# An image's group norm in one statistics chain, and score maxima taken from the SBUF copy

## The chip, the cores and the metric

The kernel runs on one core of one Trainium2 chip. Its time is the device time of one launch in microseconds; the median of three runs counts. In the text PE is TensorE (matmuls; it loads its weights beside them), DVE is VectorE, ACT is ScalarE, POOL is GpSimd and SP is SyncE, which here only starts transfers. A transfer can also be started from ACT's queue. Each engine works off its own instructions in order and waits on semaphores for the others. SBUF is the working memory of 128 partitions, PSUM holds what matmuls write.

## The reference

Two layers in float32 on an image batch x of 4 x 512 x 32 x 32. The first is a state-space layer; the change does not touch it. The second, cut to what matters (`hw` is 1024):

```python
def _gn(v, G=32, eps=1e-5):                    # group norm: 16 channels x 1024 pixels a group
    g = v.reshape(B_, G, C_ // G, H_, W_)
    m = jnp.mean(g, axis=(2, 3, 4), keepdims=True)
    s = jnp.var(g, axis=(2, 3, 4), keepdims=True)
    return ((g - m) / jnp.sqrt(s + eps)).reshape(v.shape)

def _L1_conv_ref(x, ...):                      # x is already normed by _gn
    x_top    = _conv(x, w_top, b_top, 0)       # 1x1 convolution to 64 channels
    x_center = _conv(x, w_center, b_center, 0) # 1x1 convolution to 64 channels
    x_bottom = _conv(x, w_bottom, b_bottom, 1) # 3x3 convolution, 512 to 512 channels
    ...
    sp_map = jnp.einsum('bnp,bpm->bnm', x_center, x_top)              # 1024 x 1024 scores
    sp_map = jax.nn.softmax(sp_map.reshape(bsz, -1), axis=1)          # one softmax an image
    sp_map = jnp.einsum('bnm,bmc->bnc', sp_map.reshape(...), x_bottom)
    sp_map = sp_map.reshape(bsz, c, h, w)
    return _conv(x + sp_map, w_out, b_out, 1)  # 3x3 convolution, 512 to 512 channels

x = x + _L1_conv_ref(_gn(x), ...)
```

The softmax runs over all scores of an image, so one maximum over 1024 x 1024 values is needed before any of its exponentials.

## The kernel before

The second layer works image by image. `norm` makes the normed image `xg`, `scores` the exponentials `st` of the scores, `conv3` a 3x3 convolution (with weights transformed beforehand, 24 matmul groups named (p, q) for p in 0 to 5 and q in 0 to 3, whose weight tile of 1 MB is loaded for each), `attend` the product of the two, `finish` the sum with the layer's input and the store. The statements are issued by a scheduler that orders each engine's instructions by when their inputs should be there, so that parts that don't depend on each other are interleaved. A pool gives out its tiles by tag in a ring of `bufs` buffers; a new tile waits until the last use of the one it replaces.

The order of an image's stages:

```python
xg = norm(0)
st, rz = scores(0, xg)
for b in range(B):
    xb = conv3(f"b{b}", xg, ub, brow[0])
    after = norm(b + 1) if b + 1 < B else None
    attend(b, xg, st, rz, xb)
    if after is not None:
        st, rz = scores(b + 1, after)
    finish(b, conv3(f"o{b}", xg, uo, brow[1]))
    xg = after
```

The statistics. `chunks` is a list of channel chunks of 128 partitions, `gm_sb` a matrix that averages over the 16 partitions of a group:

```python
def rsqrt(out, var):
    nc.scalar.activation(out, var, AF.Ln, bias=eps)                      # L219
    nc.scalar.activation(out, out, AF.Exp, scale=-0.5)                   # L220

def group_stats(name, chunks, psum, tag):
    n = len(chunks)
    mv = spool.tile([P, n, 2], F32, tag="mv", ...)
    for j, parts in enumerate(chunks):
        bs = spool.tile([P, len(parts), 6], F32, tag="bs", ...)
        for k, part in enumerate(parts):
            nc.vector.bn_stats(bs[:, k, :], part)                        # L229
        nc.vector.bn_aggr(mv[:, j, :], bs)                               # L230
    ...
    pm = psum.tile([P, 512], F32, tag=tag, ...)
    nc.tensor.matmul(pm[:, :n], gm_sb, mv[:, :, 0], start=True, stop=True)   # L235
    nc.vector.tensor_copy(mean, pm[:, :n])                               # L236 gmean
    nc.vector.tensor_sub(dev, mv[:, :, 0], mean)                         # L237 gdev
    nc.vector.tensor_mul(dev, dev, dev)                                  # L238
    nc.vector.tensor_add(dev, dev, mv[:, :, 1])                          # L239
    pv = psum.tile([P, 512], F32, tag=tag, ...)
    nc.tensor.matmul(pv[:, :n], gm_sb, dev, start=True, stop=True)       # L241
    rsqrt(rstd, pv[:, :n])
    return mean, rstd
```

The pools, the norm and the scores of the second layer:

```python
ps = ... tile_pool(name="l1ps", bufs=3, space=PSUM)     # tag "ps": scores, attend, pm, pv, pz
pm = ... tile_pool(name="l1pm", bufs=5, space=PSUM)     # tag "m": the convolutions
xp = ... tile_pool(name="l1x", bufs=2)
fp = ... tile_pool(name="l1f", bufs=3)

def norm(b):
    xg = xp.tile([P, NCC, HH + 2, WW + 2], F32, tag="xg", ...)
    # ... four memsets of the border on POOL ...
    for c in range(NCC):                                                 # NCC = 4
        t = fp.tile([P, L], F32, tag="f4", name=f"x1t_{b}_{c}")          # L = 1024
        for h in range(NH):                                              # NH = 2, T = 512
            nc.scalar.dma_start(                                         # L1046
                t[:, h * T : (h + 1) * T], x1[b][h][c * P : (c + 1) * P, :])
        mean, rstd = group_stats(
            f"l1_{b}_{c}", [[t[:, h * T : (h + 1) * T] for h in range(NH)]], ps, "ps")
        nc.vector.tensor_scalar(                                         # L1052
            xg[:, c, 1 : HH + 1, 1 : WW + 1], ..., mean[:, 0:1], rstd[:, 0:1],
            ALU.subtract, ALU.mult)
    return xg

def scores(b, xg):
    top = fp.tile([PAB, L], F32, tag="f4", ...)
    center = fp.tile([PAB, L], F32, tag="f4", ...)
    # ... 2 x 4 matmuls pt (L1067), copied to center and top by ACT (L1072, L1079) ...
    mx = spool.tile([P, 2 * NMC], F32, tag="mx", ...)                    # NMC = 8
    st = []
    for m in range(NMC):
        t = xp.tile([P, L], F32, tag="st", name=f"st_{b}_{m}", bufs=NMC)
        for h in range(NH):
            pt = ps.tile([P, T], F32, tag="ps", name=f"psc_{b}_{m}_{h}")
            nc.tensor.matmul(pt, top[...], center[...], ...)             # L1088
            nc.scalar.copy(t[:, h * T : (h + 1) * T], pt)                # L1092
            nc.vector.reduce_max(mx[:, 2 * m + h : 2 * m + h + 1], pt, axis=AX.X)   # L1093
        st.append(t)
    nc.vector.reduce_max(mp, mx, axis=AX.X)                              # L1096
    nc.gpsimd.partition_all_reduce(ma, mp, P, bass_isa.ReduceOp.max)     # L1098
    nc.vector.tensor_scalar_mul(ma, ma, -1.0)                            # L1099
    for m in range(NMC):
        nc.scalar.activation(st[m], st[m], AF.Exp, bias=ma,
                             accum_out=rs[:, m : m + 1])                 # L1102
    nc.vector.reduce_sum(rp, rs, axis=AX.X)                              # L1106
    nc.tensor.matmul(pt[:, 0:1], ones, rp, start=True, stop=True)        # L1108 pz
    nc.vector.reciprocal(rz, pt[:, 0:1])                                 # L1110
    return st, rz
```

The convolution, cut to what shares buffers and engines with these:

```python
for pair in PAIRS:                              # (1, 2), (3, 4), (0, 5)
    r = inputs(pair)                            # rr: row transform on POOL, ACT and DVE (L1133 to L1155)
    v = xp.tile([P, NQ, 2, NCC, P], F32, tag="v", name=f"v_{name}_{pair[0]}", bufs=2)
    # ... four DVE tensor_tensor of 128x1024 (L1169 to L1172), one for each q, in the order 2, 1, 0, 3
    for k, p in enumerate(pair):
        for q in (2, 1, 0, 3):
            w = fp.tile([P, NCC, C], F32, tag="u", ..., bufs=3)
            nc.sync.dma_start(w, u[q][p])       # L1178, 1 MB
            m[q] = pm.tile([P, C], F32, tag="m", ...)
            for c in range(NCC):
                nc.tensor.matmul(m[q], v[:, q, k, c, :], w[:, c, :], ...)    # L1182
            # ... for (1, 1) one more with the bias row (L1187) ...
        # ... m[2] is read by ACT (e, L1190), the other three by four DVE instructions (n, L1198)
    # ... POOL adds and subtracts the n of the pair into y (L1202, L1203, L1209, L1210, L1217),
    #     after pair (3, 4) also three DVE instructions (L1218 to L1220)
```

`attend` multiplies `st` with the convolution's y (pat, L1230: 8 groups of 8 matmuls into tag "ps"), and DVE adds each group to `xg` (L1236).

Of the kernel before, what the change touches and what calls it, by code (L numbers as in the profile page):

```python
# [8 lines left out]
F32 = mybir.dt.float32  # L9
AF = mybir.ActivationFunctionType  # L10
ALU = mybir.AluOpType
AX = mybir.AxisListType
# [3 lines left out]
P = 128  # L16
B, C, HH, WW = 4, 512, 32, 32
L = HH * WW
NCC = C // P
# [4 lines left out]
T = 512  # L24
NH = L // T
# [135 lines left out]
def mamba_then_pab_kernel(  # L161
# [25 lines left out]
    nc = tc.nc  # L187
# [3 lines left out]
    spool = ctx.enter_context(tc.tile_pool(name="spool", bufs=2))  # L191
# [20 lines left out]
    x1 = [  # L212
        [dram.tile([C, T], F32, tag=f"x1_{b}_{h}", name=f"x1_{b}_{h}") for h in range(NH)]
        for b in range(B)
# [10 lines that stand above are left out]
        mv = spool.tile([P, n, 2], F32, tag="mv", name=f"mv_{name}")  # L225
        for j, parts in enumerate(chunks):
            bs = spool.tile([P, len(parts), 6], F32, tag="bs", name=f"bs_{name}_{j}")
# [3 lines that stand above are left out]
        mean = spool.tile([P, n], F32, tag="gmean", name=f"gmean_{name}")  # L231
        rstd = spool.tile([P, n], F32, tag="grstd", name=f"grstd_{name}")
        dev = spool.tile([P, n], F32, tag="gdev", name=f"gdev_{name}")
        pm = psum.tile([P, 512], F32, tag=tag, name=f"pm_{name}")
        nc.tensor.matmul(pm[:, :n], gm_sb, mv[:, :, 0], start=True, stop=True)  # L235
        nc.vector.tensor_copy(mean, pm[:, :n])  # L236
        nc.vector.tensor_sub(dev, mv[:, :, 0], mean)  # L237
        nc.vector.tensor_mul(dev, dev, dev)  # L238
        nc.vector.tensor_add(dev, dev, mv[:, :, 1])  # L239
        pv = psum.tile([P, 512], F32, tag=tag, name=f"pv_{name}")  # L240
# [3 lines that stand above are left out]
# [759 lines left out]
    with ExitStack() as l1:  # L1003
        ps = l1.enter_context(tc.tile_pool(name="l1ps", bufs=3, space=PSUM))
# [9 lines left out]
        xp = l1.enter_context(tc.tile_pool(name="l1x", bufs=2))  # L1014
        fp = l1.enter_context(tc.tile_pool(name="l1f", bufs=3))
# [3 lines left out]
        for name, src in (("b", b_bottom), ("o", b_out)):  # L1019
            t = wp.tile([1, C], F32, tag=f"brow_{name}", name=f"brow_{name}")  # L1020
# [12 lines left out]
        NMC = L // P  # L1033
        HR = T // WW

        def norm(b):

            xg = xp.tile([P, NCC, HH + 2, WW + 2], F32, tag="xg", name=f"xg_{b}")
            nc.gpsimd.memset(xg[:, :, 0, :], 0.0)
            nc.gpsimd.memset(xg[:, :, HH + 1, :], 0.0)  # L1040
            nc.gpsimd.memset(xg[:, :, 1 : HH + 1, 0], 0.0)
            nc.gpsimd.memset(xg[:, :, 1 : HH + 1, WW + 1], 0.0)
            for c in range(NCC):
                t = fp.tile([P, L], F32, tag="f4", name=f"x1t_{b}_{c}")
                for h in range(NH):
                    nc.scalar.dma_start(  # L1046
                        t[:, h * T : (h + 1) * T], x1[b][h][c * P : (c + 1) * P, :]
                    )
                mean, rstd = group_stats(
                    f"l1_{b}_{c}", [[t[:, h * T : (h + 1) * T] for h in range(NH)]], ps, "ps"  # L1050
                )
                nc.vector.tensor_scalar(  # L1052
                    xg[:, c, 1 : HH + 1, 1 : WW + 1],
                    t.rearrange("p (h w) -> p h w", w=WW),
                    mean[:, 0:1], rstd[:, 0:1], ALU.subtract, ALU.mult,
                )
            return xg

        def scores(b, xg):


            top = fp.tile([PAB, L], F32, tag="f4", name=f"top_{b}")
            center = fp.tile([PAB, L], F32, tag="f4", name=f"center_{b}")
            for h in range(NH):
                pt = ps.tile([P, T], F32, tag="ps", name=f"pt_{b}_{h}")
                for c in range(NCC):
                    nc.tensor.matmul(  # L1067
                        pt, wt_sb[:, c].rearrange("p j n -> p (j n)"),
                        xg[:, c, 1 + h * HR : 1 + (h + 1) * HR, 1 : WW + 1],
                        start=(c == 0), stop=(c == NCC - 1),  # L1070
                    )
                nc.scalar.activation(  # L1072
                    center[:, h * T : (h + 1) * T], pt[PAB:P], AF.Identity, bias=bt_sb[PAB:P]
                )
                tv = top.rearrange("p (r k i j) -> p r i j k", r=4, k=2, j=TJ)
                pv = pt[0:PAB].rearrange("p (i r j k) -> p r i j k", r=4, j=TJ, k=2)
                hi = slice(h * TI // 2, (h + 1) * TI // 2)
                for r in range(4):
                    nc.scalar.activation(  # L1079
                        tv[:, r, hi], pv[:, r], AF.Identity, bias=bt_sb[0:PAB]  # L1080
                    )
            mx = spool.tile([P, 2 * NMC], F32, tag="mx", name=f"mx_{b}")
            st = []
            for m in range(NMC):
                t = xp.tile([P, L], F32, tag="st", name=f"st_{b}_{m}", bufs=NMC)
                for h in range(NH):
                    pt = ps.tile([P, T], F32, tag="ps", name=f"psc_{b}_{m}_{h}")
                    nc.tensor.matmul(  # L1088
                        pt, top[:, m * P : (m + 1) * P], center[:, h * T : (h + 1) * T],
                        start=True, stop=True,  # L1090
                    )
                    nc.scalar.copy(t[:, h * T : (h + 1) * T], pt)  # L1092
                    nc.vector.reduce_max(mx[:, 2 * m + h : 2 * m + h + 1], pt, axis=AX.X)  # L1093
                st.append(t)
            mp = spool.tile([P, 1], F32, tag="mp", name=f"mp_{b}")
            nc.vector.reduce_max(mp, mx, axis=AX.X)  # L1096
            ma = spool.tile([P, 1], F32, tag="ma", name=f"ma_{b}")
            nc.gpsimd.partition_all_reduce(ma, mp, P, bass_isa.ReduceOp.max)  # L1098
            nc.vector.tensor_scalar_mul(ma, ma, -1.0)  # L1099
            rs = spool.tile([P, NMC], F32, tag="rs", name=f"rs_{b}")  # L1100
            for m in range(NMC):
                nc.scalar.activation(  # L1102
                    st[m], st[m], AF.Exp, bias=ma, accum_out=rs[:, m : m + 1]
                )
            rp = spool.tile([P, 1], F32, tag="rp", name=f"rp_{b}")
            nc.vector.reduce_sum(rp, rs, axis=AX.X)  # L1106
            pt = ps.tile([P, T], F32, tag="ps", name=f"pz_{b}")
            nc.tensor.matmul(pt[:, 0:1], ones, rp, start=True, stop=True)  # L1108
            rz = spool.tile([P, 1], F32, tag="rz", name=f"rz_{b}")
            nc.vector.reciprocal(rz, pt[:, 0:1])  # L1110
            return st, rz
# [129 lines left out]
        def finish(b, y):  # L1241

            dst = out[b].rearrange("(c p) h w -> p c (h w)", p=P)
            for j in range(NCC):
# [19 lines left out]
                nc.scalar.dma_start(dst[:, j, :], o)  # L1264
# [11 lines that stand above are left out]
# [57 lines left out]
```

## Time and profile before

| | |
|---|---|
| median of three runs | 3682.53 us (3678.94 to 3693.1) |
| span of the profiled execution | 3679.3 us |
| first layer | up to about 2450 us |
| second layer | about 1230 us, four images |
| busy over the span: PE, DVE, POOL, ACT | 81%, 67%, 57%, 51% |
| score matmuls psc (L1088), passes x mean | 128 x 0.993 us |
| maxima from PSUM mx (L1093) | 64 x 0.688 us |
| copies st (L1092) | 64 x 0.585 us |
| bn_stats (L229), second layer | 32 x 0.680 us |
| normalisations xg (L1052) | 16 x 0.815 us |
| table loads at L219 and L220, second layer | 15 and 15, mean 1.283 us |

The profile is that of one execution. A group of instructions is named by line, engine, operation and tile, written as out<-in. A float32 matmul stands in it as two passes, so "x768" are 384 matmuls. "Idle before, releaser" says how long an engine stood still ahead of a group, and what ended that. The chain of waits follows the end of the program back from step to step to what released it; it is printed here in order of time. A busy share over the whole span mixes the two layers, so a stage is read from the chain and from the timeline of that stage.

### The profile page before, as it was taken

To read this page: it belongs to the slowest core of one execution; us is meant where nothing else is said; L and a number is where in the kernel's file an instruction comes from. 1 tells how busy PE (TensorE), PEld (TensorE's weight loads), DVE (VectorE), ACT (ScalarE), POOL (GpSimd) and SP (SyncE) were. 2 spreads that over 40 slices of the span, in tenths; PEclk is the share of its full clock that TensorE was granted. 3 is DMA by queue.
4 is the path that set the end of the run, shared out by engine and by line. 5 is a ranking of instruction groups with operands and counts; after the bars stand their busy time and mean duration, and the time that the engine had idled before them with its cause. 6 is when DMAs were issued, how large, how long until landed. Compare 5 with 4: busy or idle time off the path is not lost.

```text
span 3679.3 us, 34763 instructions
## 1 busy us (share of the span) xinstructions
PE 2993.7 (81%) x11208; PEld 1733.5 (47%) x11208; DVE 2465.7 (67%) x2115; ACT 1885.5 (51%) x3567; POOL 2085.2 (57%) x1006
## 2 busy tenths in 40 slices
PE   5878788886688877787887867759889889989988
PEld 3355545554455555445555555523334334434434
DVE  3567878785999987779987788925246435425524
ACT  3487878775768786577775687712130111012000
POOL 6699977685676687666676698912122113113221
PEclk9888898988899888888888988877879979988999
DMA  7588667787667788757777788844418607806817
GB/s 225 171 288 292 231 207 241 242 293 250 231 220 237 246 302 283 244 173 244 255 258 247 276 285 293 302 146 154 149 67 321 228 12 282 316 7 220 331 67 255
DMA packets 378509, 836.38 MB, mean 227 GB/s; under 512 B 33560, under 2 KB 205848, under 8 KB 353496
## 3 DMA queue, kind: packets, MB, share of 16 engines
q1 hardware_dynamic: 367024, 816.50, 64.5%
q10 hardware_dynamic: 11304, 17.67, 1.4%
q8 instruction: 89, 1.46, 0.2%
q14 instruction: 92, 0.75, 0.1%
HBM read 726.57 MB, written 107.48 MB: 227 GB/s over the span
## 4 chain that ended last, share of the span: by engine, by line
PE 46%; DVE 20%; POOL 12%; issue 9%; ACT 7%; DMA 5%; SPq 0%; ACTq 0%; POOLq 0%; DVEq 0%
PE m_o L1182 9%; PE m_b L1182 9%; PE pat L1230 6%; PE y L788 5%; PE po L347 5%; DVE da L768 4%; POOL da L780 3%; PE u L739 3%; PE psc L1088 3%; POOL bbc L754 3%; PE pz L347 3%; DVE bbc L768 2%; PE pxm L347 2%; DVE u L768 2%; ACT sc L725 2%
## 5 line engine op out<-in xcount | busy, mean ns | idle before, releaser
L780 POOL TENSOR_TENSOR da<-da,cbc 128x1024 f32<-128x1024 f32 x256 | 608.5, 2378 | 292.6 <-DVE da L768 244.8
L725 ACT ACTIVATE sc<-dtxt,bt_sb 128x128 f32<-128x128 f32 x2048 | 633.1, 389 | 112.8 <-PE u L739 112.0
L768 DVE TENSOR_TENSOR_SCAN da<-da,u 128x1024 f32<-128x1024 f32 x256 | 582.3, 2275 | 150.4 <-PE u L739 134.6
L754 POOL TENSOR_TENSOR bbc<-dtx,bbc 128x1024 f32<-128x1024 f32 x256 | 607.2, 2382 | 110.2 <-DMA bbc<-bcd 99.9
L739 PE MATMUL u<-ident,sc 128*128 128x128 f32 x2048 | 318.2, 306 | 123.7 <-DVE da L768 72.7
L788 PE MATMUL y<-ident,bbc 128*128 128x128 f32 x2048 | 321.3, 308 | 114.7 <-DVE bbc L775 79.1
L788 PE MATMUL y<-ident,da 128*128 128x128 f32 x2048 | 321.5, 307 | 113.1 <-POOL da L780 109.9
L1182 PE MATMUL m_o<-uw_o,v_o 128*128 128x512 f32 x768 | 354.9, 622 | 23.8 <-DVE v_o L1169 23.2
L788 PEld LDWEIGHTS y<-ident,da 128*128 128x128 f32 x2048 | 270.3, 160 | 198.4 <-POOL da L780 156.2
L780 POOL TENSOR_TENSOR bbc<-bbc,cbc 128x1024 f32<-128x1024 f32 x128 | 306.0, 2391 | 101.2 <-DVE bbc L768 96.8
L733 ACT ACTIVATE da<-dt,a_sb 128x1024 f32<-128x1024 f32 x256 | 290.7, 1140 | 140.0 <-PE y L788 135.7
L788 PEld LDWEIGHTS y<-ident,bbc 128*128 128x128 f32 x2048 | 273.9, 160 | 185.7 <-DVE bbc L775 95.9
L739 PEld LDWEIGHTS u<-ident,sc 128*128 128x128 f32 x2048 | 270.9, 159 | 180.6 <-issue 77.9
L1182 PE MATMUL m_b<-uw_b,v_b 128*128 128x512 f32 x768 | 340.0, 602 | 6.1 <-DVE v_b L1169 5.1
L760 ACT ACTIVATE u<-dt,a_sb 128x1024 f32<-128x1024 f32 x256 | 284.4, 1111 | 113.1 <-DVE da L768 66.5
L768 DVE TENSOR_TENSOR_SCAN bbc<-u,bbc 128x1024 f32<-128x1024 f32 x128 | 292.0, 2281 | 54.9 <-ACT u L760 33.0
L768 DVE TENSOR_TENSOR_SCAN u<-u,bbc 128x1024 f32<-128x1024 f32 x128 | 292.1, 2282 | 41.3 <-POOL bbc L754 25.3
L347 PE MATMUL po<-gt,wpr 128*128 128x512 f32 x512 | 242.9, 626 | 31.1 <-DMA wt_sb<-in_w_center_dram 15.4
L347 PE MATMUL pz<-xt,winc 128*128 128x512 f32 x512 | 249.9, 626 | 10.5 <-ACT dt L676 5.5
L1182 PEld LDWEIGHTS m_o<-uw_o,v_o 128*128 128x128 f32 x768 | 149.3, 198 | 226.0 <-issue 195.3
L1182 PEld LDWEIGHTS m_b<-uw_b,v_b 128*128 128x128 f32 x768 | 145.6, 192 | 192.8 <-issue 183.8
L1230 PE MATMUL pat<-y_b,st 128*128 128x512 f32 x512 | 228.4, 609 | 0.0
(214 smaller groups left out, 4116.1 us busy)
## 6 DMA issues: line engine op xcount, KB each, us to landing
cbc<-bcd SPq DMA_DIRECT2D x512, 512.0 KB, 5.5
bbc<-bcd SPq DMA_DIRECT2D x256, 512.0 KB, 5.9
uw_b<-u_b SPq DMA_DIRECT2D x96, 1024.0 KB, 4.8
uw_o<-u_o SPq DMA_DIRECT2D x96, 1024.0 KB, 4.7
szd<-sz SPq DMA_DIRECT2D x32, 512.0 KB, 5.9
szl<-szd SPq DMA_DIRECT2D x32, 512.0 KB, 7.0
gd<-szl SPq DMA_DIRECT2D x32, 512.0 KB, 5.8
winc<-wind SPq DMA_DIRECT2D x56, 256.0 KB, 4.5
```

The costliest lines, as they stand in the source:

```text
L347: lambda k=k, lhs=lhs, rhs=rhs: nc.tensor.matmul(p(), lhs(), rhs(), start=(k == 0), stop=(k == n - 1)),
L725: nc.scalar.activation(sc()[:, k, :], dtxt()[:, k, :], AF.Copy, scale=bt()[:, k, s : s + 1],)
L733: lambda: nc.scalar.activation(da(), dt(), AF.Exp, scale=scale),
L739: nc.tensor.transpose(u()[:, k * P : (k + 1) * P], sc()[:, k, :], ident)
L754: "POOL", 2.35, lambda: nc.gpsimd.tensor_mul(dbx(), dtx(), b_bc()),
L760: lambda: nc.scalar.activation(da(), dt(), AF.Exp, scale=scale),
L768: lambda: nc.vector.tensor_tensor_scan(ht(), da(), dbx(), 0.0, ALU.mult, ALU.add),
L780: "POOL", 2.35, lambda: nc.gpsimd.tensor_mul(hc(), ht(), c_bc()),
L788: nc.tensor.matmul(y[h]()[:, k, :], hc()[:, at * P : (at + 1) * P], ident, start=(s == 0 and k == 0), stop=(s == NS - 1 and k == NK - 1), ...
L1088: nc.tensor.matmul(pt, top[:, m * P : (m + 1) * P], center[:, h * T : (h + 1) * T], start=True, stop=True,)
L1182: nc.tensor.matmul(m[q], v[:, q, k, c, :], w[:, c, :], start=(c == 0), stop=(c == NCC - 1 and not extra),)
L1230: nc.tensor.matmul(pt, st[m][:, 2 * P * j + h : 2 * P * (j + 1) : 2], xb[m // 2][:, m % 2, :], start=(m == 0), stop=(m == NMC - 1),)
```

## The change

The statistics of an image's four channel chunks go through one chain (one mean matmul, one variance matmul, one Ln and one Exp for four columns) where there were four chains of one column. All of the image is loaded ahead of it, into one tile of 128 x 4 x 1024, which has the size of a transformed-input tile of the convolution and takes a buffer of that ring (tag "v", two buffers) instead of four tiles of the ring "f4". And the maxima of the scores are taken from the copy in SBUF, 1024 columns at a time, so that a PSUM buffer of the scores has only one reader. It is meant to shorten the waits of TensorE around the norm and the scores. The diff:

```diff
+            t = xp.tile([P, NCC, L], F32, tag="v", name=f"x1t_{b}")
             for c in range(NCC):
-                t = fp.tile([P, L], F32, tag="f4", name=f"x1t_{b}_{c}")
                 for h in range(NH):
                     nc.scalar.dma_start(
-                        t[:, h * T : (h + 1) * T], x1[b][h][c * P : (c + 1) * P, :]
-                    )
-                mean, rstd = group_stats(
-                    f"l1_{b}_{c}", [[t[:, h * T : (h + 1) * T] for h in range(NH)]], ps, "ps"
-                )
+                        t[:, c, h * T : (h + 1) * T], x1[b][h][c * P : (c + 1) * P, :]
+                    )
+            mean, rstd = group_stats(
+                f"l1_{b}",
+                [[t[:, c, h * T : (h + 1) * T] for h in range(NH)] for c in range(NCC)],
+                ps, "ps",
+            )
+            for c in range(NCC):
                 nc.vector.tensor_scalar(
                     xg[:, c, 1 : HH + 1, 1 : WW + 1],
-                    t.rearrange("p (h w) -> p h w", w=WW),
-                    mean[:, 0:1], rstd[:, 0:1], ALU.subtract, ALU.mult,
+                    t[:, c].rearrange("p (h w) -> p h w", w=WW),
+                    mean[:, c : c + 1], rstd[:, c : c + 1], ALU.subtract, ALU.mult,
                 )
             return xg
@@ scores
-            mx = spool.tile([P, 2 * NMC], F32, tag="mx", name=f"mx_{b}")
+            mx = spool.tile([P, NMC], F32, tag="mx", name=f"mx_{b}")
@@
                     nc.scalar.copy(t[:, h * T : (h + 1) * T], pt)
-                    nc.vector.reduce_max(mx[:, 2 * m + h : 2 * m + h + 1], pt, axis=AX.X)
+                nc.vector.reduce_max(mx[:, m : m + 1], t, axis=AX.X)
                 st.append(t)
```

## The prediction

> **What bounds the kernel now.** The page's busy shares (PE 81%, DVE 67%, POOL 57%, ACT 51%) are averages over two layers with different limits, and the change touches only the second, which starts at about 2450 us. So I read the chain of waits from there to the end: start, length, engine, tile, line, count.
>
> ```profile
> 2545.78 66.34 PE m_b L1182 x154
> 2612.15 0.69 DVE n_b L1198
> 2612.94 2.34 DVE gdev_l L237
> 2615.72 0.60 PE pv_l L241 x2
> ...
> 2622.44 1.28 ACT L219
> 2624.01 1.28 ACT L220
> 2625.55 0.82 DVE xg L1052
> 2626.36 1.20 DVE bs_l L229 x2
> 2627.85 0.60 PE pm_l L235 x2
> 2629.36 0.56 PE pv_l L241 x2
> 2629.92 57.93 PE pat L1230 x128
> ...
> 2708.78 0.61 DVE mx L1093
> 2709.43 5.48 PE psc L1088 x6
> 2714.91 2.00 PE m_o L1182 x2
> ...
> 2738.88 4.90 PE m_o L1182 x8
> ...
> 3431.11 75.73 PE m_b L1182 x176
> 3506.84 54.95 PE pat L1230 x128
> ```
>
> The reader is to see three things. In the convolutions (m_b, m_o) TensorE is the bound: 0.43 us a pass, two passes a matmul, so 3.43 us for the four matmuls of one weight tile, without a gap. Between the last m_b of an image and attend's first pat lie 17.8 us (2612.12 to 2629.92) in which the four small chains of the next image's norm are worked off one after the other; the gap is 17.7 and 17.9 us for the two images after it. Image 3, which has no norm behind it, has none: m_b ends and pat starts at 3506.84. And after attend the score matmuls wait for VectorE's maxima. The timeline of that stretch (start, length, engine, line, tile; idle before it and what ended it):
>
> ```profile
> 2696.00 2.84 PE L1088 MATMUL psc<-center,top 64*128 64x512 f32 x6 [1.26 <-ACT top L1079]
> ...
> 2701.91 2.07 PE L1182 MATMUL m_o<-uw_o,v_o 128*128 128x512 f32 x2 [3.07 <-DVE v_o L1169]
> ...
> 2708.70 1.87 DVE L1093 TENSOR_REDUCE mx<-psc 128x1 f32<-128x512 f32 x3
> 2709.43 5.48 PE L1088 MATMUL psc<-center,top 64*128 64x512 f32 x6 [5.45 <-DVE mx L1093]
> ```
>
> Three scores fill the three PSUM buffers by 2698.9. ScalarE has copied them out by 2699.5, but VectorE's maxima stand behind three transforms in its queue and come at 2708.7. Only then do the buffers come free. The sixteen scores, with four matmuls of the first weight tile scattered among them, thus last until m_o's second tile at 2738.88, 51.0 us after attend's end at 2687.85.
>
> [...] the first three scores left 0.86 us apart, later ones 1.71 us, and an m_o pass after 3.07 us of idle took 1.03 us against 0.43. [...] So I give a maximum over 1024 columns in SBUF the time of a 1024-column tensor_tensor, 1.22 us with 1.15 from start to start (v_o L1169); from PSUM 512 columns took 0.69. [...] here Ln and Exp each load, 15 times each, mean 1283. [...] The windows view agrees that both fit:
>
> ```profile
> 2840.00:2850.00 10.00, 10.00 (x24) 4.26 (x23) 2.70 (x6) 0.60 (x1) 0.00 (x0) 1.00 1.02 399
> 2860.00:2911.00 51.00, 50.76 (x120) 22.34 (x118) 20.70 (x22) 3.07 (x4) 12.20 (x5) 1.00 0.85 306
> ```
>
> PE stays busy all 10 us while x1t loads of image 2 run (last three columns: PE clock, DMA share, GB/s): 399 GB/s were to be had, the weights alone take 306.
>
> **The change, part by part.**
>
> *One chain, images 1 to 3.* The order of instructions of the changed kernel puts all eight bn_stats of the next image into the last pair of the convolution before it, so after the last m_b only one pm and one pv stand before pat. pm follows at once (0.3 us); VectorE runs the last n_b (to +0.7), gmean, then gdev L237, which will still take 2.3 us because POOL's y_b runs beside it (POOL L1203 lasted from 2612.92 to 2615.26, gdev from 2612.94 to 2615.27), then two small ones; pv at +3.6, pat at about +4.1 instead of +17.8. Ln, the table load and Exp (1.8 us) and four normalisations (4 x 0.81) end at about +9.4, when the first pat group is just ready to be read; pat needs none of them. Saved: 13.7 x 3 = 41 us.
>
> *One chain, image 0.* This norm is fully exposed. The sixth half tile of the kernel before had landed by 2463.7; eight will have by about 2465. Then: last bn_stats and aggregate 0.9, pm 0.6, four small ones 0.8, pv 0.8, Ln 0.3, table load 1.3, Exp 0.2, four normalisations 3.2: about 2474 instead of 2480.2. Saved: 6 us.
>
> *Maxima over the copy.* Now only ScalarE's copy (0.58 us) frees a score buffer, so all sixteen can run at the pace of the first three, 0.86 us: 13.8 us instead of about 43. In the new order they stand in one block ahead of m_o's first tile. Counting from the end of attend (image 1): psc starts at +8.1 as before, ends at +21.9, then m_o tiles (1,2), (1,1) with its bias row (1.05), (1,0), (1,3): +36.7.
>
> There the gain is cut, because the next instruction of PE is now pz, the sum of the softmax, and pz needs everything that hangs on the maxima. VectorE, from its old times: v_o L1171 ends at +20.9; then eight maxima (1.15 each, 9.2), the fourth transform of this pair and two of the next (3 x 1.15) and two rr (2 x 1.2) up to the combined maximum at +36; POOL's all-reduce 1.24 plus hops, the sign: ma at +38; ScalarE's eight Exp at 1.13: +47.3; rp and pz: +48.1. So PE waits about 11.4 us at pz and takes up tile (2,2), the fifth of 24, at +48.1. Twenty tiles remain: 20 x 3.43 = 68.6, plus 2.3 for a cold start (17 pat passes after the long gap took 10.42 us, 7.3 at full clock, so at most 3). The convolution ends at +119.0. Before it ended at 2821.74, +133.9. Saved: 14.8 us in image 1; by the same count 15.3 and 13.8 in images 2 and 3 (134.3 and 132.9 before). In image 0 the same chain hangs on rr (2487.37 before), from where m_b's end was 124.8 us away and will be 111.1: 13.7. Sum: 57.6 us.
>
> *The load in place of a transformed tile.* x1t now takes one of the two v buffers and may be loaded once the pair (3,4) has been multiplied, 27.4 us (8 tiles) before the convolution ends. In that time 2.1 MB of x1t and 8.4 MB of weights must come, 383 GB/s, just under the 399 seen, and up to two tiles of the weights are there already. VectorE's queue has the first bn_stats ahead of y_b L1218, but L1218 waits for POOL until 5.5 us after the last n_b anyway, and a load lands in 5.0 us (median). I put 1 us per image for it: -3.
>
> Sum: 41 + 6 + 57.6 - 3 = 102 us; 3682.5 - 102 = 3580 us.
>
> **The rivals.**
>
> 1. *The scores were bound by PE, or the array goes cold.* Then sixteen scores take 16 x 1.71 = 27.4 us and end at +35.5. For it: most scores of the kernel before ran at 1.71. Against: those came after idle of 3 to 5 us, the first three, 1.3 us after other matmuls, ran at 0.86. It would cost little anyway: 13.6 us more, of which 11.4 would have been waited away at pz. About 3590.
>
> 2. *VectorE is the bound.* The maxima over SBUF are slower than I think, or the transforms collide with POOL (v_o L1170 takes 3.5 us beside POOL, 1.22 alone). Each 0.25 us on a maximum delays pz by 2 us, in four images 8 us. For it: from +21 to +38 VectorE has no idle left and sets pz. Against: POOL's work of this stretch (l, k, four memsets) is over by +20.8. At 1.7 us a maximum: about 3597.
>
> 3. *The loads arrive late.* x1t beside the weights starves PE in the last pair, or VectorE, blocked at bn_stats, holds back the PSUM buffers of m. For it: the two streams need 383 GB/s, where weights alone had 306. Against: the windows above. If PE lost 6 us an image: about 3596. If the statistics came after the last m_b, a further 5 us an image.
>
> 4. *The gaps are hidden anyway.* If something else set pat's start (y_b of POOL), the 41 us would shrink. Against: after image 3 pat follows m_b without any gap, though y_b ends at the same distance; its first six matmuls don't touch the last y_b. I give this little.
>
> **Range and chances.** Rivals 1 to 3 together would leave some 3615, each alone stays under 3600. On the other side, no cold start in pat (54.95 us without the gap against 57.2 to 57.9) and free transfers would bring 3568. Eight times in ten: 3562 to 3605. The border of 2% lies at 3609, 73 us saved; norm alone brings 47, so the scores must give 26 of the 58: 0.88. Within 2%: 0.11. Slower by 2% would need a stall that I don't see: 0.01.
>
> **What would show it.** In the chain, m_b to pat should be about 4 us, and one Ln and one Exp load an image remain (4 of each in this layer, not 15). psc should come as one block of about 14 us without a wait for mx, then about 11 us of idle PE before pz, released by rp. mx on 128x1024 should take 1.2 us. x1t loads should be issued in the last third of each m_b convolution, with m_b passes still 0.43 us apart. I would be wrong if psc waits for ScalarE's copies, if pz comes later than +50, or if weights arrive late beside x1t.

## The result, and the profile after

The changed kernel takes 3576.19 us (median of 4, 3564.93 to 3587.45), the kernel before 3682.53 (3678.94 to 3693.1) on the same chip: ratio 0.9707, 95% interval 0.9669 to 0.9744. Predicted were 3580 us, 3562 to 3605.

Medians carry the spread of the first layer, which the change does not touch: in the thirteen profiles of this study its last addition (VectorE, L886) starts anywhere from 2440.2 to 2454.3 us. So the second layer is measured below from that addition to the end of the span. The addition in the kernel before, whose span is 3679.3 us, and in the changed one, with 3577.1:

```profile
2449.35 0.69 DVE L886 TENSOR_TENSOR res<-res,po 128x512 f32<-128x512 f32 x1 [2.33 <-PE po L347]
2448.65 0.69 DVE L886 TENSOR_TENSOR res<-res,po 128x512 f32<-128x512 f32 x1 [2.23 <-PE po L347]
```

The second layer took 1229.9 us before and takes 1128.4 after: 101.5 saved, where the sum of the prediction was 102. The two kernels that were run twice agree in this measure to 0.3 us (1082.5 and 1082.8) and 0.8 us (1077.0 and 1076.1).

The chain of waits of the changed kernel, from the last matmuls of image 0's m_b to the end of the convolution m_o that follows image 1's scores (start, length, engine, tile, line, count):

```profile
2577.25 13.99 PE m_b L1185 x32
...
2591.26 0.69 DVE n_b L1201
...
2592.05 2.34 DVE gdev_l L237
...
2594.83 0.59 PE pv_l L241 x2
2595.43 57.79 PE pat L1233 x128
...
2689.18 1.25 POOL ma L1101
...
2700.14 0.59 PE pz L1111 x2
2700.72 71.78 PE m_o L1185 x160
```

The reader is to see that m_b (end 2591.24) and pat (2595.43) now lie 4.2 us apart instead of 17.8, with one gdev and one pv between them; the two later gaps are 4.0 us. And m_o is no longer followed back to a wait for maxima inside psc, but to pz, by way of the Exp's and the all-reduce. The timeline of the same stretch shows what TensorE did meanwhile, and VectorE's first maximum (idle before an instruction, and what ended it, in brackets):

```profile
2661.36 14.00 PE L1091 MATMUL psc<-center,top 64*128 64x512 f32 x32 [1.27 <-ACT top L1082]
...
2674.08 1.21 DVE L1096 TENSOR_REDUCE mx<-st 128x1 f32<-128x1024 f32 x1
...
2675.29 7.13 PE L1185 MATMUL m_o<-uw_o,v_o 128*128 128x512 f32 x16
...
2700.14 0.59 PE L1111 MATMUL pz<-rp,ones 128*128 128x1 f32 x2 [9.59 <-DVE rp L1109]
```

The sixteen scores stand in one block of 14.0 us, which begins 8.1 us after attend's end (2653.22). The first maximum starts 1.3 us before the end of the block, so no score waits for one any more. Four weight tiles of m_o follow, then 9.6 us of idle at pz, and the fifth tile starts 47.5 us after attend's end (+47.5; such times are counted from there).

The transfers of x1t, and the weights beside them, in the timeline of image 0's last pair:

```profile
2562.05 2.40 ACTq L1046 DMA_DIRECT2D x1t<-x  x5
...
2573.11 3.67 PE L1185 MATMUL m_b<-uw_b,v_b 128*128 128x512 f32 x8 [0.79 <-DMA uw_b<-u_b]
...
2577.25 13.97 PE L1185 MATMUL m_b<-uw_b,v_b 128*128 128x512 f32 x32 [0.47 <-DMA uw_b<-u_b]
```

They are issued 29.2 us before m_b's end, and TensorE waits 1.26 us for weights behind them.

### The profile page after: what moved, and what is told of

It reads as the page before. It is cut to its first block, busy times and chain, and to the rows that moved or that the text cites. A ratio compares the mean times of both kernels' runs of the same rounds, so it can differ in the third digit from the quotient of the medians.

```text
span 3577.1 us, 34547 instructions
## 1 busy us (share of the span) xinstructions
PE 2908.6 (81%) x11160; PEld 1694.8 (47%) x11160; DVE 2449.5 (68%) x2035; ACT 1857.3 (52%) x3521; POOL 2085.8 (58%) x1006
## 4 chain that ended last, share of the span: by engine, by line
PE 43%; DVE 20%; POOL 13%; DMA 8%; issue 8%; ACT 7%; SPq 1%; ACTq 0%; POOLq 0%; DVEq 0%
PE m_o L1185 8%; PE m_b L1185 8%; PE pat L1233 6%; PE po L347 5%; PE y L788 5%; POOL da L780 4%; DVE da L768 3%; PE pz L347 3%; POOL bbc L754 3%; PE u L739 3%; ACT sc L725 2%; DMA cbc<-bcd 2%; PE pxm L347 2%; DVE bbc L768 2%; POOL bbc L780 2%
## 5 line engine op out<-in xcount | busy, mean ns | idle before, releaser
L739 PE MATMUL u<-ident,sc 128*128 128x128 f32 x2048 | 316.5, 305 | 119.3 <-DVE da L768 64.6
L1185 PE MATMUL m_o<-uw_o,v_o 128*128 128x512 f32 x768 | 342.8, 608 | 14.0 <-DVE v_o L1172 14.0
L768 DVE TENSOR_TENSOR_SCAN u<-u,bbc 128x1024 f32<-128x1024 f32 x128 | 292.1, 2282 | 39.4 <-POOL bbc L754 17.8
```

The lines of the kernel that those rows point to most:

```text
L739: nc.tensor.transpose(u()[:, k * P : (k + 1) * P], sc()[:, k, :], ident)
L768: lambda: nc.vector.tensor_tensor_scan(ht(), da(), dbx(), 0.0, ALU.mult, ALU.add),
L1185: nc.tensor.matmul(m[q], v[:, q, k, c, :], w[:, c, :], start=(c == 0), stop=(c == NCC - 1 and not extra),)
```

## The experiments

**The two parts alone.** The first run has the one chain and the load in a v tile, with the maxima still taken from PSUM; the second the four chains of before, with the maxima over the copy. The edit of each against the changed kernel, the parts taken back:

```diff
 # run 1
-                nc.vector.reduce_max(mx[:, m : m + 1], t, axis=AX.X)
+                    nc.vector.reduce_max(mx[:, 2 * m + h : 2 * m + h + 1], pt, axis=AX.X)
 # run 2
-            t = xp.tile([P, NCC, L], F32, tag="v", name=f"x1t_{b}")
             for c in range(NCC):
+                t = fp.tile([P, L], F32, tag="f4", name=f"x1t_{b}_{c}")
 ...             # load, group_stats and normalisation of one chunk, four times
```

Expected of run 1: 

> Norm part alone (one statistics chain in the v buffer), maxima from PSUM as in the kernel before. If the two parts add up: gap from the last m_b to pat 4.2 us instead of 17.8 in three images (41 us), first norm 7 us earlier, about 1.3 us an image lost to weights that come late beside x1t: 3682.5 - 44 = 3638 us, and psc still waits for mx. Rival, that the norm only pays because the scores behind it got shorter (or that they hide one another): under 20 us saved, above 3660.

Expected of run 2: 

> Maxima over the SBUF copy alone, norm with its four chains as before. If the parts add up: 13 to 15.5 us from attend's end to the end of the convolution in each of four images, 57 us: 3626 us, the 17.8 us gap before pat still there, PE idle about 10 us before pz. Rival, that the gain comes from the norm tile leaving the f4 ring: under 30 us saved, above 3650.

Measured: run 1 3638.59 us, ratio 0.9856 (0.9835 to 0.9878); run 2 3624.21, ratio 0.9818 (0.9797 to 0.984). In the second layer the norm saves 43.9 us (1186.0), which is the prediction's 41 + 6 - 3, and the maxima 61.0 (1168.9), against 57.6. The two come to 104.9 where the change as a whole saves 101.5. So they add up but for 3.4 us. TensorE's waits for weights of m_b sum to 1.1 us before, 1.9 in run 2, 6.5 in run 1 and 4.2 after; they do not explain the difference, since without them it would be larger, and it stays open. Neither part alone is shown to bring 2%, the change as a whole does, and neither gain hides the other.

**The sum of the softmax behind the convolution.** Is the idle time at pz really on the path, or would TensorE have had to wait for something else there? rp, pz and rz are taken out of `scores` and issued just ahead of `attend`, the first place where rz is needed; the arithmetic is the same.

```diff
-            return st, rz
+            return st, rs
+        def total(b, rs):       # rp, pz, rz as before
-            attend(b, xg, st, rz, xb)
+            attend(b, xg, st, total(b, rs), xb)
```

Expected: 

> The changed kernel with the sum of the softmax (rp, pz, rz) issued only after the convolution that follows the scores. If PE's wait at pz is on the path: the 9.6 us of idle and about 3 us of cold start after it go, in four images, 50 us less: about 3528 us, m_o tiles following one another right behind psc. Rival, VectorE is the bound there and the wait moves to the PSUM buffers of m or to the next transforms: under 15 us less, above 3560.

Measured: 3531.7 us (3524.52 to 3542.88), ratio 0.9584 (0.9559 to 0.9608). Its chain of waits over the same stretch as above:

```profile
2575.40 0.59 PE pv_l L241 x2
2575.99 0.42 PE pz L1115 x2
2576.42 57.75 PE pat L1237 x128
...
2642.33 14.00 PE psc L1091 x32
...
2664.44 75.75 PE m_o L1189 x176
```

From attend to the end of m_o there is now nothing but TensorE in the chain, apart from 1.2 us of ScalarE's copies to center and top ahead of psc: no maxima, no all-reduce, no Exp. pz costs 0.42 us where it stands now. The second layer is 45.9 us shorter than the changed kernel's. From attend's end to m_o's end images 1 to 3 (counted by their scores) take 106.0 us each in place of 118.8 to 119.3: the wait at pz (9.6 us), pz itself (0.6), and some 3 us because m_o no longer starts again with slow passes. (In the changed kernel the granted clock is 0.50 from pz until 2706.6, and seven passes of m_o take 0.8 to 1.0 us each, which is what is meant by a cold start below; here the 176 passes behind psc take 75.75 us, 0.43 each.) With 11.0 us in image 0 that makes 50 us, of which some 4 are lost again in other stretches. The wait was real, and the change had only moved it there from psc.

**Each maximum taken twice.** If the chain from the maxima to pz sets the end, as rival 2 has it, 9 us more of maxima an image should show in full.

```diff
-                nc.vector.reduce_max(mx[:, m : m + 1], t, axis=AX.X)
+                for k in range(2):
+                    nc.vector.reduce_max(mx[:, 2 * m + k : 2 * m + k + 1], t, axis=AX.X)
```

Expected: 

> The changed kernel with every maximum taken twice over the same SBUF tile (one more VectorE instruction of 1.13 us for each of eight tiles). The order of instructions then has pz one and a half weight tiles later. If VectorE's maxima set pz: ma 9 us later, rp and pz 9 us later, of which 5 us are filled with the tiles now ahead of pz: 4 us an image, 3576 + 16 = 3592 us. Rival, pz is set by something else (ScalarE's copies, POOL): ma does not move, and the time stays or falls by up to 20 us because pz stands later.

Measured: 3567.73 us (3564.65 to 3571.57), ratio 0.9672 (0.9654 to 0.969); the second layer even 10.1 us shorter than the changed kernel's. A miss: the time fell, as under the rival, though the maximum did come later. The timeline of image 1, VectorE and TensorE, each from its own view:

```profile
2666.87 18.11 DVE L1097 TENSOR_REDUCE mx<-st 128x1 f32<-128x1024 f32 x16
```

```profile
2686.16 10.24 PE L1186 MATMUL m_o<-uw_o,v_o 128*128 128x512 f32 x20 [6.26 <-DVE v_o L1176]
2697.14 0.38 PE L1112 MATMUL pz<-rp,ones 128*128 128x1 f32 x2 [0.73 <-DVE rp L1110]
```

The edit had changed the order too. All sixteen maxima now stand in one block ahead of the fourth transform, the two rr and the next pair's transforms, and POOL's all-reduce took 0.38 us here instead of 1.24, so the maximum was ready only 3.5 us later instead of 9; and pz stands six matmuls (5.15 us) later in TensorE's order. pz itself came 4.2 us later after attend's end than in the changed kernel, but by then TensorE had done 5.15 us more of the convolution: it stood idle for 7.0 us in two waits (6.26 for v_o, 0.73 at pz) in place of 9.6. From attend's end to m_o's end images 1 to 3 are 3.3 to 4.2 us shorter, of which these 2.6 are a part. The run therefore says nothing on the cost of a maximum. The order of the maxima and transforms on VectorE and the place of pz on TensorE had changed with it and more than made up for it; which of them did so was not tried apart.

**A longer chain in the same order.** To lengthen the chain alone, POOL's all-reduce is repeated on its own result, which leaves the value as it is: four times more, and 24 times more.

```diff
             nc.gpsimd.partition_all_reduce(ma, mp, P, bass_isa.ReduceOp.max)
+            for _ in range(4):          # 24 in the second run
+                nc.gpsimd.partition_all_reduce(ma, ma, P, bass_isa.ReduceOp.max)
```

Expected of four more: 

> The changed kernel with POOL's all-reduce of the maximum done five times in a row in place of once (the same result; the order of instructions on TensorE and VectorE stays exactly that of the changed kernel, which the run with doubled maxima did not keep). One takes 1.24 us with about 0.05 to 0.1 between two: ma comes about 5.2 us later. Theory (the chain maxima, ma, Exp, rp, pz sets when m_o goes on, in all four images, m_b in image 0): TensorE's wait before pz grows from 9.6 to about 14.8 us, and the time by 4 x 5.2 = 21 us, to 3597, ratio about 0.976. Rival (some other thing than this chain holds TensorE there, or the delay is taken up later, as the run with doubled maxima let one think): the time grows by less than 8 us.

Expected of 24 more: 

> The all-reduce of the maximum 25 times in a row. In the run with five, the four further ones took 0.35 us each, not 1.24, and 0.445 from one to the next: the chain grew by 1.78 us and the wait at pz by 1.76. Twenty-four further ones make it 10.7 us longer. The order of instructions now puts pz one weight tile later (3.43 us) in images 1 to 3 and three of four matmuls later (2.6 us) in image 0. Theory (what hangs on the maximum holds TensorE at pz one to one, less what the order lets it do before): the wait at pz is 9.6 + 10.7 - 3.4 = 16.9 us in images 1 to 3, and the time 3 x 7.3 + 8.1 = 30 us more than the changed kernel's, 3606, ratio 0.979. Rival (the chain isn't what holds TensorE): less than 12 us more.

Measured, four more: 3582.22 us, ratio 0.9718 (0.9694 to 0.9742). That is far from the 3597 expected, and by its number alone the rival's. But the groups of the profile show that a repeated all-reduce is not the first one's size:

```profile
L1103 POOL PARTITION_ALL_REDUCE ma<-ma x16: 350/350/351, 2506.8 to 3240.1; - x16
L1101 POOL PARTITION_ALL_REDUCE ma<-mp x4: 1237/1237/1238, 2505.4 to 3237.4; - x4
```

(The columns after the count are the shortest, median and longest in ns.) The chain grew by 1.78 us, not 5.2, and TensorE's timeline has the wait at pz grown by 1.76, to 11.35. Over the four images the waits at pz sum to 44.5 us instead of 37.3. Not all of that reaches m_o's end, which comes 0.9, 0.9 and 0.4 us later after attend's end in images 1 to 3: the 160 passes behind pz took 70.9, 70.4 and 70.4 us instead of 71.8, 71.3 and 71.8, with five slow passes at the start in image 1 instead of seven. The second layer is 8.8 us longer, and its waits for weights are 3.4 us more than the changed kernel's (7.6 and 4.2).

Measured, 24 more: 3607.97 us (3605.83 to 3617.16), ratio 0.9797 (0.978 to 0.9815), against 3606 expected.

```profile
2715.11 0.59 PE L1113 MATMUL pz<-rp,ones 128*128 128x1 f32 x2 [18.82 <-DVE rp L1111]
```

The chain grew by 12.7 us rather than 10.7 (the first all-reduce took 2.37 us here, and the others stand 0.48 apart in the mean). One tile of 3.43 us was done ahead of pz, so the wait should be 9.6 + 12.7 - 3.4 = 18.9, and is 18.82, as the timeline line above has it. The second layer is 38.2 us longer, and the waits at pz are 38.0 longer in sum (75.3 against 37.3). That the two agree is in part chance: m_o's end comes 7.9 to 8.1 us later in images 1 to 3 and not 9.2, for the slow passes behind pz were again fewer, and the waits for weights are 3.4 us more (7.6 and 4.2). By the medians the kernel is 31.8 us slower, near the 30 expected; in the profiled run (3609.22 us) the first layer ended 8 us earlier than in the changed kernel's profile (L886 at 2440.6 against 2448.7). With this the doubt that the doubled maxima had left is settled: what delays the maximum delays pz, and with it the fifth tile, one to one, less what the order puts ahead of pz. Of the longer wait, 8.0 of 9.2 us reach m_o's end here, and 0.4 to 0.9 of 1.8 with four more.

**Half of the load.** Only 512 of the 1024 columns of each channel chunk are loaded, and used for both halves. This leaves out half of the norm's input.

```diff
-                for h in range(NH):
-                    nc.scalar.dma_start(t[:, c, h * T : (h + 1) * T], ...)
+                nc.scalar.dma_start(t[:, c, 0:T], x1[b][0][c * P : (c + 1) * P, :])
```

Expected: 

> The changed kernel with half the load of x1t: only the first 512 columns of each channel chunk are brought in, and used for both halves (the computation leaves out half of the input of the norm; the instructions on VectorE, and their sizes, are nearly as before). Theory: the short waits of TensorE for weights in the last pair of m_b (1.26 us in the stretch from image 0 to 1, from 0.79 and 0.47) are x1t's transfers getting ahead of the weights; with half the bytes they should shrink to under 0.4 us an image. The first norm, which waits for the last x1t transfer, should have its normalised tile 2 to 3 us earlier than 2472.2. The gap from m_b to pat stays at 4.0 to 4.2 us, since it hangs on VectorE's last n_b and gdev and not on the load. Rival: the waits are the weights' own (the same streams in all convolutions), then they stay at about 1.3 us. Time about 3570 us by theory (2.5 + 3 less), 3576 by the rival.

Measured: 3580.48 us in one run; the second layer is 2.0 us longer than the changed kernel's. Mostly a miss. Behind the x1t loads the waits for weights are 0, 0.52 and 0 us in images 0 to 2, where the changed kernel had 1.26, 0.45 and 1.75. Those of images 0 and 2 are gone, as they would be if they came from the load; but they are absent too in images 0 and 2 of a kernel with the full load (the first profile under "Both" below), so this is not shown. And waits of 1.97, 1.14 and 1.05 us appeared at the beginning of m_b, 35 to 40 us ahead of x1t's loads, and the sum over the layer rose from 4.2 to 6.0. The first norm became no earlier, but, counted from L886, 1.7 us later. A window of the first norm's load says why, columns as in the prediction's (DMA share and GB/s last); this is the run with half the load:

```profile
2456.00:2458.00 2.00, 0.00 (x0) 0.00 (x0) 0.00 (x0) 0.00 (x0) 0.00 (x0) 0.50 1.03 427
```

The DMA engines are as busy in either kernel (share 1.03 and 427 GB/s here, 1.06 and 441 in the same two microseconds of the changed kernel), as the first weight tiles of m_b are loaded at the same time. Halving x1t let the weights' loads be issued sooner (three within 1.3 us instead of 9.0), and VectorE's last wait for x1t still ended at 2463.0. Besides, the normalisation in eight pieces took 3.74 us instead of 3.0. What x1t costs over the whole layer is thus not settled: the waits for weights vary between 1 and 8 us from kernel to kernel, and that is more than the cost in question. They are 1.1 and 1.9 us in the two kernels with four chains and 3.3 to 7.6 in the eleven with one, so the norm part does bring more of them; but image 3, which loads no x1t, has some too (0.7 us in the changed kernel), so x1t's bytes are not all of it.

**The norm one tile group earlier.** A gap of 4 us was left, with a cold start of pat behind it (a granted clock of 0.52 in its first 5.6 us in the changed kernel). `norm(b + 1)` is issued just ahead of m_b's last tile group (5, 0), so that pm and pv stand within it.

```diff
+                        if hook and (p, q) == (5, 0):
+                            hook()                    # norm(b + 1)
-            after = norm(b + 1) if b + 1 < B else None
```

Expected: 

> The changed kernel with the next image's norm placed one weight tile group earlier: pm and pv stand ahead of and within m_b's last tiles (5,x), so that pat follows the last m_b directly. Theory: the remaining gap of 4.0 to 4.2 us between m_b and pat, and with it the cold start of pat (57.79, 56.75, 56.76 us against 54.95 without a gap, about 2.1 on average), are still on the path. Removing both brings (4.1 + 2.1) x 3 = 18 us, less about 1 us of stall in all for pm and pv in the middle of m_b: about 3559, ratio 0.966 to 0.967. Rival (y_b of POOL, or the last n_b, sets pat's start anyway): the gap stays at 3 us or more and the time within 4 us of 3576. Second rival: pm waits for statistics that come late and stalls m_b by more than 4 us an image; then the time is 3576 or more.

Measured: 3558.99 us (3556.41 to 3564.96), ratio 0.9656 (0.9632 to 0.9681). The chain of waits:

```profile
2569.62 7.10 PE m_b L1187 x16
2576.72 0.12 PE pm_l L235 x2
2576.84 2.68 PE m_b L1187 x6
2579.52 0.12 PE pv_l L241 x2
2579.64 4.40 PE m_b L1187 x10
2584.04 54.95 PE pat L1235 x128
```

pm and pv cost 0.12 us each between matmuls, pat follows m_b at once and takes 54.95 us, the time without a cold start. The gap, and the cold start behind it, had been on the path.

**Both.** The early norm and the late sum together, and then both this kernel and the one with the late sum alone once more on one chip (the edits are those above).

Expected of both: 

> The early norm together with the sum of the softmax moved behind the convolution (the run with rp, pz and rz just before attend had 3531.7 us). Theory: the two gains lie in different stretches and add: 3531.7 - 17 = 3515 us, ratio about 0.954. Rival: pz, which now stands just before attend, waits or stalls together with pv, or the gap comes back as a wait for rz; then at most the gain of one of the two remains, 3530 or more.

Expected of the late sum again: 

> The kernel with the sum of the softmax after the convolution once more, beside the next one on the same chip. Theory: as before, about 0.958 of the kernel before; no wait at pz, psc in blocks of 14.0 us.

Expected of both again: 

> The early norm and the late sum together once more, on the same chip as the run before. In its first profile one of the four blocks of scores ran at a granted clock of 0.55 and took 25.27 us in place of 14.0, with the first sixteen matmuls of m_o after it 9.4 in place of 7.1; nothing behind absorbed these 13.5 us, so the run of 3524.7 would have had 3511 without it. Theory: the gains add, and what is missing comes from such blocks: the median is 8 to 17 us under that of the run with the late sum alone (ratio 0.953 to 0.956), and the profile has (its time - 3511) / 13.5 slow blocks. Rival: the early norm brings nothing once pz is late; then the two are within 3 us.

Measured: both 3523.49 us, ratio 0.9563 (0.9523 to 0.9604), then 3520.73 (3504.08 to 3532.2), ratio 0.9542 (0.952 to 0.9564). The late sum alone had 0.9584, then 3531.42 and 0.9578 (0.9556 to 0.9601). The second pair differs by 10.7 us, within the 8 to 17 expected and short of the 17 that the parts promise. TensorE's timeline of the repeat shows where the rest is:

```profile
2901.61 25.95 PE L1091 MATMUL psc<-center,top 64*128 64x512 f32 x32 [1.26 <-ACT top L1082]
2927.49 8.71 PE L1191 MATMUL m_o<-uw_o,v_o 128*128 128x512 f32 x16
```

And the windows of an image's scores before it, and of this block (the value before the DMA share is the granted clock of TensorE):

```profile
2649.70:2663.70 14.00, 14.00 (x33) 5.98 (x33) 13.97 (x7) 9.48 (x18) 10.08 (x7) 1.00 0.00 0
2901.60:2927.60 26.00, 25.99 (x33) 9.86 (x33) 25.39 (x16) 9.50 (x19) 10.07 (x7) 0.53 0.00 0
```

The same 32 passes took 26 us instead of 14, at a clock of 0.53, and m_o's first sixteen 8.71 instead of 7.1. In both profiles of this kernel one block in four did so. From attend's end to m_o's end that image took 119.5 us where the other two with scores there took 106.0 to 106.3. The second layer took 1077.0 and 1076.1 us; without these 13.5 us it would be 1063, which is 65 less than the changed kernel, and the late sum (45.9) and the early norm (14.3, and some 1 more for the half-clock block in its own profile, see below under rival 1) give 61. The 4 us between are of the size of the waits for weights, which are 6.4 us with the early norm alone and 3.3 and 4.5 here. So the gains add, and a half-clock block takes part of it. The version with both beats the kernel before and the changed one.

The second half of what was expected of the repeat does not hold: by its time its profile, at 3532.2 us, should have had 1.6 such blocks, and had one. The rest is the first layer, which ended last of all there (2454.3).

## Why the prediction was right

*One chain, images 1 to 3.* Right, step by step: gdev took 2.34 us beside POOL's y_b (2.34 us from 2592.03), pv came 3.6 us after m_b's end and pat 4.2 after it, where 3.6 and 4.1 had been said. Saved 13.6 to 13.9 us each. The cold start was rightly left in the sum: pat took 57.79, 56.75 and 56.76 us. One Ln and one Exp load an image remain.

*One chain, image 0.* The normalised tile was ready at 2472.2 us, not 2474, and the first score starts 6.7 us earlier after L886 (32.0 against 38.7); 6 were predicted.

*Maxima over the copy.* The path and nearly all sizes held: psc in one block of 14.0 us (13.8), mx 1.21 us (1.22, an estimate from the 1.22 us of a transform of 1024 columns), the fifth tile at +47.5 (+48.1), m_o's end at +119.3, +118.8 and +119.3 (+119.0). In image 0, rr to m_b's end took 111.8 us (111.1). The wait at pz was 9.6 us and not 11.4, since the four tiles before it ended at +37.3 and not +36.7, pz was over at +47.5 and not +48.1, and the 11.4 held pz's own 0.6 as well. The end at +119.3 owes something to luck: the 160 passes behind pz took 71.8 us where 70.9 had been counted (68.6 and 2.3 for the cold start), which the earlier pz made up for in part. From these ends the four images saved 14.6, 15.5, 13.6 and 13.0 us, 56.7 against 57.6.

*The load.* 1 us an image was said; 1.26, 0.45 and 1.75 us of waits lie behind the loads. Their place was right. The reason given, 383 GB/s wanted against 399 seen in one window, is consistent with it but not shown by it; with half the load two of these waits were gone, and the sum of such waits was not smaller.

*The rivals.* Rival 1 did not decide the changed kernel: all four blocks of its profile ran at full clock. But it exists: 3 of the 44 blocks of this form in the profiles ran at about half clock (25.2 to 26.0 us in place of 14.0). Where pz stands behind the scores, the wait swallows most of it, as the rival said: with the early norm alone, the one half-clock block (25.23 us) left no wait at pz, and the fifth tile started at +50.8, 3.3 us late. m_o's end came at +119.8, only 1.1 us after that of the other two images, since no cold start followed (the 40 passes behind pz took 17.41 us, 0.44 each). Rival 2, VectorE as the bound, was half right: its chain does set pz, one to one, but the maxima are as fast as was thought. Rivals 3 and 4 fell with the 4 us gap and with the early norm.

*What the prediction did not see.* It took pz as given. Moving three small instructions brought 45.9 us in the second layer, nearly half of the 101.5 that the whole change had brought.

## What to carry to other kernels

When a wait on a slow engine is taken out of a stage, follow that engine's result to its next reader on the bound engine: a small matmul placed early in the bound engine's order takes over the wait (pz, 9.6 us an image here), so place it where its result is first needed. To lengthen a chain as a test, compare the order of instructions first, because a scheduler may answer a costlier instruction with another order, and then the run measures that. Measure a change in its own stage, from an instruction ahead of it, when the rest of the kernel spreads by as much as the effect.

## What was not expected of the hardware

A block of 25.99 us of TensorE work in a stretch of 26.0 ran at a mean granted clock of 0.53. The windows of it, and of m_o's start behind it, show that the clock was full at first and fell while TensorE was busy (the clock is again the value before the DMA share):

```profile
2901.60:2903.30 1.70, 1.69 (x4) 0.86 (x5) 1.70 (x1) 1.24 (x4) 1.70 (x1) 1.00 0.00 0
2903.40:2927.40 24.00, 24.00 (x29) 8.89 (x27) 23.59 (x16) 8.20 (x14) 8.27 (x7) 0.50 0.00 0
2927.50:2930.60 3.10, 3.10 (x5) 1.50 (x5) 2.38 (x4) 0.59 (x1) 0.00 (x0) 0.50 0.69 195
2930.70:2936.00 5.30, 5.30 (x13) 2.10 (x11) 4.85 (x5) 3.20 (x6) 1.24 (x1) 1.00 0.57 210
```

For 24.0 us TensorE worked without a gap (24.00 busy in the second window), and the clock stayed at 0.50. These matmuls use 64 of the 128 rows (64\*128 in the line), and m_o, with all 128, came back to full clock within its first sixteen passes: 3.2 us after its start here, and by estimate 4.7 and 4.6 us in the other two cases (from a mean clock of 0.76 over 9.5 us, and from 9.43 us for sixteen passes in place of 7.13). All three such blocks were in the three profiles with the early norm (3 of 12, against 0 of 32 in the others). Whether the rows or the early norm is the cause was not tried.

A repeated all-reduce on POOL took 0.35 us after a first one of 1.24. But being the first is not what makes it long: with the maxima taken twice, the only all-reduce of an image took 0.38 us, and with 24 more behind it the first took 2.37. What sets its time was not tried.

And four short chained instructions on 4 columns decided a gap of 4 us because one of them, gdev, took 2.33 us while POOL's addition of the same length ran beside it:

```profile
2592.03 2.34 POOL L1206 TENSOR_TENSOR y_b<-y_b,n_b 128x1024 f32<-128x1024 f32 x1 [7.52 <-DVE gmean_l L236]
2592.05 2.33 DVE L237 TENSOR_TENSOR gdev_l<-mv_l,gmean_l 128x4 f32<-128x4 f32 x1
```

In the thirteen profiles, each of the 30 gdev of the second layer that ran beside this addition took 2.33 to 2.34 us, and each of the others, the early norm's among them, 0.15 to 0.16.
